# Shift columns in 128-column tiles, and their transpose behind the other pieces of a half step

## The chip, the cores and the metric

The kernel runs on one core of a Trainium2 chip. The core has five engines that run side by side and meet at semaphores: TensorE (PE, matrix products and transposes, with its weight loads PEld), VectorE (DVE), ScalarE (ACT), GpSimd (POOL) and SyncE (SP, which here only issues DMA transfers). The on-chip memory SBUF holds operands; results of TensorE go to PSUM[...]. The metric is the device time of one execution, in microseconds (us), as the median of several runs. Less is better.

## The reference

The input has 8 batches of 512 tokens of width 128. A layernorm is followed by two branches whose results are added to the input: a differential attention with 8 heads, and a mixture of 8 experts of which each token uses two, plus a shared expert.

```python
xn = _layernorm(x)
# attention: two softmaxes per head, each over scores of width F = 8
scores = jnp.einsum('bqhif,bkhif->ibhqk', qs, ks_) * scale
atts = jax.nn.softmax(scores, axis=-1)
att = atts[0] - diff_weight * atts[1]
o = jnp.einsum('bhqk,bkhe->bqhe', att, vs)
normed = (o * rsqrt(mean(o * o) + eps) * norm_w).reshape(b, s, e)
attn = (normed @ Wo.T + bo) * (1.0 - diff_weight)
# experts
gates = jax.nn.sigmoid(xf @ Wg)
vals, idx = jax.lax.top_k(gates, 2)          # then normalized to sum 1
shared = silu(xf @ Ws1) * (xf @ Ws3) @ Ws2
h = silu(einsum('td,edf->tef', xf, We1)) * einsum('td,edf->tef', xf, We3)
routed = einsum('tef,efd,te->td', h, We2, w)
x = x + attn + (shared + routed) / 3
```

A softmax needs the largest score of each row subtracted before the exponential. That maximum is the "shift" of this document.

## The kernel before

**Layout.** For each batch, `qst` and `kst` hold the queries and keys of all heads, stacked in 64 rows per softmax, in two buffers that alternate by batch. Each number is split into an upper and a lower part, and two more rows of `qst` (from row `SHIFT`) hold the negated maximum of every query, so that the product of `kst` and `qst` comes out of TensorE already shifted.

**The main loop** (from line 1066 on) runs over 8 batches x 4 pairs of heads x 4 tiles of 128 keys: 128 steps of two halves. A half step issues, in this order:

1. `scores` (line 764 on): two matmuls into `sc`, which has one PSUM buffer, and ScalarE's exponential, `pe<-sc`.
2. `next_maxima(1)` (line 961): one tile of `maxima`, which runs twelve tiles ahead: two matmuls into `mx` (line 731, one PSUM buffer) and VectorE's `most<-mx` (line 738). Behind the eighth tile of a pair of heads VectorE makes `parts` (lines 741 to 745): the maxima split into an upper and a lower part, 32 columns in all, by four small operations.
3. Transfers that lie ready: an "errand" (a gather or scatter of the experts on GpSimd), a copy into `qst` or `kst`, or the load of an expert's weights.
4. In the first half of a step: `pieces(step)` and then those parts that a piece marked "soon". In the second half: the parts marked "late" and then `weigh`, eight matmuls into `av`.

**Pieces.** All other work is cut into jobs, each a Python generator: the routing, the experts (`pxq`, `ph`, `py`), the shared expert (`ps`), the preparation of a later batch (`px`, `pq`, `pv`), `fold` (`po`), `conclude` (`pn`, `pz`) and `shift` (line 749). A job states for its next piece what it costs and how many PSUM banks it needs. `pieces` (line 1038) sorts the jobs by due time, those with `must` ahead of all, and starts each that still fits: it calls `j.go()`, which issues the piece, and lowers what is left of the room (2.25) and of the three banks of `small_psum`. Only the `shift` jobs have `must`. A bank goes to the tile that asks for it next, and the instruction that first writes it waits until the tile before it has been read. Each engine runs its own instructions in the order in which they were issued.

**The shift.** `shift(b, w)` transposes the 32 columns of `parts` (line 754, `pm`); "late", ScalarE copies the 32 rows to SBUF (line 757, `rows`), and SyncE issues two transfers into rows of `qst` (line 759). They have to be there when the scores of that pair of heads begin, two steps after the piece.

**The rest that the change touches.** `early` takes tiles out of the pool `p12` (twelve wide buffers, tag "w"), which later holds the weights of the experts. `zeros` (line 138) is the source of three small transfers, and `before` (line 938) is a triangular matrix for counting. At the end of the run `combine(b)` loads two results for each token of a batch (`ym`, line 638), adds them to `r` (eight operations of line 647 for each batch), and `settle` stores `r` to the output (line 613, by SyncE) as soon as both sums of a batch are there.

Of the kernel before, what the change touches and what calls it, by code (L numbers as in the profile page):

```python
# [11 lines left out]
F32 = mybir.dt.float32  # L12
# [7 lines left out]
P = 128  # L20
# [11 lines left out]
def kernel(  # L32
# [52 lines left out]
    nc = tc.nc  # L85
    B, S, E = x.shape
    NT = S // P
    NE, _, FF = We1.shape
# [32 lines left out]
    def early(name, *widths):  # L121
        t = p12.tile([P, WIDE], F32, tag="w", name=name)
        begin = [sum(widths[:i]) for i in range(len(widths) + 1)]
        return [t[:, i:j] for i, j in zip(begin, begin[1:])]
# [10 lines left out]
    make_identity(nc, ident)  # L135
    minus_half = const.tile([P, NT], F32, name="minus_half")
    nc.gpsimd.memset(minus_half, -0.5)
    zeros = const.tile([P, E], F32, name="zeros")
    nc.gpsimd.memset(zeros, 0.0)
    wg = const.tile([P, NE], F32, name="wg")  # L140
    nc.sync.dma_start(out=wg, in_=Wg)
# [35 lines left out]
    for i in range(2):  # L177
        vals.append(const.tile([P, NT, H, 32], F32, name=f"vals{i}"))
        qst.append(const.tile([P, H, S], F32R, name=f"qst{i}"))
        kst.append(const.tile([P, H, S], F32R, name=f"kst{i}"))  # L180
    nc.vector.memset(kst[0].bitcast(F32), 1.0)
    nc.gpsimd.memset(qst[0].bitcast(F32), 0.0)

    def later_constants():
# [536 lines left out]
    def maxima(b, w):  # L721

        q, k = qst[b % 2], kst[b % 2]
        most = p2.tile([P, NT, 2, 2], F32, tag="most", name=f"most_{b}_{w}")
        for u in range(2):
            for t in range(NT):
                free = (b, w) == (0, 0) or (b, w, u) == (0, 1, 0)
                tag = "sc" if free and t % 2 else "mx"
                sc = ps_1.tile([P, 2, S], F32, tag=tag, name=f"mx_{b}_{w}_{u}_{t}")
                for i in range(2):  # L730
                    nc.tensor.matmul(  # L731
                        sc[:, i, :],
                        q[ROWS[i], 2 * w + u, t * P : (t + 1) * P],
                        k[ROWS[i], 2 * w + u, :],
                        start=True,
                        stop=True,
                    )
                nc.vector.tensor_reduce(most[:, t, u, :], sc, AX.X, ALU.max, negate=True)  # L738
                latest[:] = [most[0:1, t, u, :]]
                yield  # L740
        parts = p2.tile([P, 2, 2, 2, NT], F32, tag="parts", name=f"parts_{b}_{w}")
        for i in range(2):
            m = most[:, :, :, i].rearrange("p t u -> p u t")
            nc.vector.tensor_copy(parts[:, i, 0].bitcast(F32R), m)
            nc.vector.tensor_tensor(parts[:, i, 1], m, parts[:, i, 0], ALU.subtract)  # L745
        n = 2 * 2 * 2 * NT
        state[b]["parts", w] = parts.rearrange("p i l u t -> p (i l u t)"), n

    def shift(b, w):
        q = qst[b % 2]  # L750
        yield 0.25, 1
        parts, n = state[b].pop(("parts", w))
        pm = small_psum(f"pm_{b}_{w}")
        nc.tensor.transpose(pm[:n, :P], parts, ident)
        yield "late"
        rows = p2.tile([n, P], F32, tag="rows", name=f"rows_{b}_{w}")
        nc.scalar.copy(rows, pm[:n, :P])
        for i in range(2):
            nc.sync.dma_start(
                out=q[64 * i + SHIFT : 64 * i + SHIFT + 2, 2 * w : 2 * w + 2, :].bitcast(F32),  # L760
                in_=rows[n // 2 * i : n // 2 * (i + 1), :],
            )
# [172 lines left out]
            pass  # L935


    before = const.tile([P, P], F32, name="before")
    counted = {}

    def count_up():
# [31 lines left out]
    with tc.manual_schedule():  # L973
        norms = {b: norm(b) for b in range(B)}
        next(norms[0])

        pw = small_psum("pw")
        for i in range(4):
            nc.tensor.transpose(pw[:, i * P : (i + 1) * P], w_raw[:, i, :], ident)

        w_c = const.tile([P, 2, 2, F, H], F32, name="w_c")
        for i in range(2):
            nc.vector.tensor_copy(
                w_c[:, i],
                pw[:, i * P : (i + 1) * P].rearrange("p (u i f) -> p i f u", i=2, f=F),
            )
        w_t = const.tile([P, 2, E], F32, name="w_t")
        nc.scalar.copy(w_t.rearrange("p i e -> p (i e)"), pw[:, 2 * P :])
        run(norms[0])
        first = prepare(0)  # L990
        next(first)
        next(first)
        next(first)
        next(norms[1])
        next(first)
        later_constants()
        run(norms[1])
        px = {1: turn(1)}
        next(norms[2])
        next(first)  # L1000
        next(first)
        run(norms[2])
        run(first)
        later_loads()
        count_up()
        gates(0, state[0]["xnT"])
        for b in range(1, B):
            xnT, p = px.pop(b)
            nc.scalar.copy(xnT, p)
            if b + 2 < B:  # L1010
                next(norms[b + 2])
            if b + 1 < B:
                px[b + 1] = turn(b + 1)
            if b + 2 < B:
                run(norms[b + 2])
            gates(b, xnT)
        nc.scalar.activation(gate.rearrange("p t e -> p (t e)"), pg, AF.Exp, scale=-1.0)
        next_maxima(8)
        run(shift(0, 0))
        sides = const.tile([P, 1], F32, name="sides")  # L1020
        nc.vector.memset(sides, 1.0)
        for i in (32, 96):
            nc.vector.tensor_scalar(sides[i : i + DH], dw[i : i + DH], -1.0, None, ALU.mult)
        keep = const.tile([P, 1], F32, name="keep")
        nc.vector.tensor_scalar(keep, dw, -1.0, 1.0, ALU.mult, ALU.add)
        nw_s = const.tile([P, 1], F32, name="nw_s")
        nc.vector.tensor_scalar(nw_s, nw, keep, None, ALU.mult)
        nc.gpsimd.tensor_scalar(bo_b, bo_b, keep, None, ALU.mult)
        nc.gpsimd.tensor_scalar(s2, s2, OUT_SCALE, None, ALU.mult)
        nc.gpsimd.memset(qst[1].bitcast(F32), 0.0)  # L1030
        nc.gpsimd.memset(kst[1].bitcast(F32), 1.0)
        for b in range(B):
            loads.append(lambda b=b: keep_tokens(b))
        for e in range(NE):
            loads.append(lambda e=e: keep_expert(e))
        next_maxima(AHEAD - 8)

        def pieces(step):

            room, banks = ROOM if step < total else 99.0, BANKS - len(held)  # L1040
            begun = []
            for j in sorted(jobs, key=lambda j: (not j.must, j.last - j.left, j.first)):
                if step < j.first or (j.next is None and not j.ready()):
                    continue
                j.next = j.next or next(j.part)
                cost, need = j.next
                late = step > j.last - j.left
                if need > banks or (cost > room + 0.5 * late and cost > 0 and not (late and begun == [])):
                    continue
                j.go()  # L1050
                room -= cost
                banks -= need
                begun.append(j)
            return begun

        def follow(begun, when):
            for j in begun:
                if j.next == when:
                    j.go()
                    if j.next is None:  # L1060
                        jobs.remove(j)

        total = STEPS * B
        pes = last = None
        step = 0
        while step < total + 1 or jobs or errands or loads:
            for second_half in range(2):
                if step < total:
                    b, r = divmod(step, STEPS)
                    w, c = divmod(r, NT)  # L1070
                    pe = scores(b, w, c, second_half)
                    pes = [pe] if not second_half else pes + [pe]
                next_maxima(1)
                turns += 1
                if errands:

                    if latest:
                        nc.gpsimd.tensor_copy(mark, latest.pop())  # L1078
                    errands.popleft()()

                if copies and (turns % 4 or not loads):
                    copies.popleft()()
                elif loads:
                    loads.popleft()()
                if not second_half:
                    begun = pieces(step)
                    follow(begun, "soon")
                else:
                    follow(begun, "late")
                    if last is not None:  # L1090
                        weigh(*last)
                    last = (b, w, c, pes) if step < total else None
            step += 1
# [48 lines left out]
```

## Time and profile before

| | |
|---|---|
| median of 3 runs | 703.55 us (701.72 to 706.61) |
| the profiled execution | 702.99 us |
| its span, first to last instruction | 701.1 us |
| mean granted TensorE clock | 0.926 of full speed |
| `pm` (line 754): weight load / matmul | 32 x 94 ns / 32 x 283 to 395 ns |
| `parts` (lines 744, 745), each | 64 x 161 to 184 ns, 64 x 166 to 171 ns |
| `rows<-pm` (line 757) | 32 x 238 to 255 ns |
| `most<-mx` (line 738) | 256 x 1222 ns |
| `pe<-sc` (line 776) | 256 x 1024 ns |

A line of the profile's groups names the source line, the engine, the operation and the tiles, output first: `pm<-ident,parts` is the transpose into `pm`. For matmuls "128\*32" means 128 rows by 32 columns of the array. In views that run in order of time the first number is the start in us from the beginning of the span, the second the duration; in brackets stands how long the engine had been idle and which instruction released it. An engine followed by q (SPq) is its instruction queue, here the issue of a transfer. Ends of matmuls are modelled, starts are recorded; so distances between starts are the safer measure.

The maxima's own work is large (312.1 us of VectorE's 500.3), and the shift is small: 32 transposes, 9.2 us of TensorE in all.

### The profile page before, as it was taken

Reading aid. Unit: us, or ns where it says so; the run is one execution under the profiler, and the core shown is the slowest. Engines: PE = TensorE matmul, PEld = TensorE weight load, DVE = VectorE, ACT = ScalarE, POOL = GpSimd, SP = SyncE. Lnnn points to the kernel's source line nnn. Section 1 sums busy time; section 2 is a strip of 40 time slices with the busy share of each in tenths; the row PEclk is TensorE's granted clock in tenths of the full one; section 3 lists DMA queues with packets and bytes.
Section 4 is the critical chain, followed back from the end, with each engine's and each line's share of the span. In section 5 each row is a group of like instructions: output and inputs, shape, how many; then the busy total and the mean of one; then the engine's idle time right before and its main releaser. Section 6 shows DMA issues by size and latency. Waiting matters only on the chain.

```text
span 701.1 us, 10912 instructions
## 1 busy us (share of the span) xinstructions
PE 619.3 (88%) x3788; PEld 329.0 (47%) x3788; DVE 500.3 (71%) x836; ACT 376.2 (54%) x554; POOL 264.1 (38%) x440
## 2 busy tenths in 40 slices
PE   4867768898989999999999999999999999996654
PEld 2733213444525555556545655455555555453113
DVE  7678877678677767867787666777777777777820
ACT  1204425446455675567566755566566666574442
POOL 6313008654034443545245344434544253332000
PEclk9556978999999999999999998999999999998877
DMA  5302313203143344324442444323433444013510
GB/s 163 120 1 90 122 69 93 68 19 122 47 152 111 107 127 145 125 66 136 135 163 77 136 154 143 110 65 105 141 114 112 122 145 114 17 32 114 179 69 16
DMA packets 38696, 72.64 MB, mean 104 GB/s; under 512 B 6489, under 2 KB 12762, under 8 KB 38618
## 3 DMA queue, kind: packets, MB, share of 16 engines
q1 hardware_dynamic: 33026, 61.07, 26.8%
q0 software_dynamic: 4608, 9.45, 4.3%
q10 hardware_dynamic: 1008, 1.44, 0.7%
q8 instruction: 30, 0.49, 0.3%
q14 instruction: 24, 0.20, 0.1%
HBM read 45.68 MB, written 12.09 MB: 82 GB/s over the span
## 4 chain that ended last, share of the span: by engine, by line
PE 66%; DVE 22%; ACT 5%; issue 3%; DMA 2%; POOL 1%; SPq 0%; POOLq 0%; ACTq 0%; DVEq 0%
PE sc L768 12%; PE av L787 12%; DVE most L738 11%; PE ph L570 10%; PE mx L731 8%; PE py L583 5%; PE ps L809 4%; PE pz L877 3%; ACT pe L776 3%; PE pi L393 2%; PE pq L663 2%; PE pg L235 2%; DVE r L647 2%; PE px L225 1%; DVE parts L745 1%
## 5 line engine op out<-in xcount | busy, mean ns | idle before, releaser
L738 DVE TENSOR_REDUCE most<-mx 128x2 f32<-128x1024 f32 x256 | 312.1, 1222 | 119.9 <-PE mx L731 112.9
L776 ACT ACTIVATE pe<-sc 128x1024 f32<-128x1024 f32 x256 | 262.2, 1024 | 221.0 <-PE sc L768 214.6
L768 PE MATMUL sc<-qst,kst 64*128 64x512 f32 x512 | 132.2, 512 | 21.2 <-ACT pe L776 13.9
L787 PE MATMUL av<-pe,vals 128*32 128x512 f32 x1024 | 142.9, 631 | 0.0
L731 PE MATMUL mx<-kst,qst 64*128 64x512 f32 x512 | 123.6, 478 | 14.6 <-DVE most L738 14.5
L768 PEld LDWEIGHTS sc<-qst,kst 64*128 64x128 f32 x512 | 49.2, 188 | 172.0 <-ACT pe L776 119.6
L507 POOL DMA_INDIRECT xq<-tokens,tokens_at x72 | 71.2, 989 | 37.1 <-issue 27.8
L595 POOL DMA_INDIRECT results<-y,results_at x72 | 70.9, 984 | 35.1 <-issue 29.0
L1078 POOL COPY mark<-most 1x2 f32<-1x2 f32 x144 | 25.4, 176 | 149.9 <-DVE most L738 143.8
L570 PE MATMUL ph<-xT,w 128*128 128x128 f32 x576 | 74.4, 283 | 1.5 <-DVE r L881 0.9
L731 PEld LDWEIGHTS mx<-kst,qst 64*128 64x128 f32 x512 | 51.6, 197 | 47.7 <-DVE most L738 45.8
L570 PEld LDWEIGHTS ph<-xT,w 128*128 128x128 f32 x576 | 68.5, 195 | 8.1 <-issue 5.9
L838 POOL TENSOR_TENSOR o<-on 128x128 f32<-128x128 f32 x32 | 14.7, 461 | 142.4 <-DVE on L834 142.0
L787 PEld LDWEIGHTS av<-pe,vals 128*32 128x32 f32 x1024 | 20.7, 109 | 45.6 <-issue 45.4
L809 PE MATMUL ps<-xnT,s 128*128 128x512 f32 x64 | 33.8, 641 | 6.6 <-DVE th_s L544 3.0
L544 DVE SCALAR_TENSOR_TENSOR th<-th,ph 128x512 f32<-128x512 f32 x36 | 24.8, 688 | 19.9 <-ACT th L543 14.2
L583 PE MATMUL py<-w,h 128*128 128x128 f32 x288 | 37.3, 281 | 1.5 <-DVE h L547 0.9
L583 PEld LDWEIGHTS py<-w,h 128*128 128x128 f32 x288 | 33.7, 191 | 5.7 <-issue 3.2
L543 ACT ACTIVATE th<-ph 128x512 f32<-128x512 f32 x36 | 21.5, 597 | 18.8 <-PE ph L570 16.1
L797 ACT ACTIVATE ov<-av,sides 128x512 f32<-128x512 f32 x32 | 22.2, 695 | 12.9 <-PE av L787 12.7
L429 POOL TENSOR_SCALAR here<-numbers,inner 128x128 f32<-128x128 f32 x32 | 19.9, 621 | 15.8 <-DVE inner L381 15.8
L547 DVE TENSOR_TENSOR h<-th,ph 128x512 f32<-128x512 f32 x36 | 24.4, 678 | 0.0
(137 smaller groups left out, 599.0 us busy)
## 6 DMA issues: line engine op xcount, KB each, us to landing
w<-experts SPq DMA_DIRECT2D x72, 384.0 KB
qst<-upper SPq DMA_DIRECT2D x32, 128.0 KB
qst<-lower SPq DMA_DIRECT2D x32, 128.0 KB
kst<-lower SPq DMA_DIRECT2D x32, 128.0 KB
ym<-results SPq DMA_DIRECT2D x16, 256.0 KB
kst<-upper SPq DMA_DIRECT2D x28, 128.0 KB
experts<-in_L_ffn_We_dram SPq DMA_DIRECT2D x24, 128.0 KB
tokens<-xn SPq DMA_DIRECT2D x8, 256.0 KB
```

The lines of the kernel that those rows point to most:

```text
L507: nc.gpsimd.indirect_dma_start(out=xq[:, n, :], out_offset=None, in_=tokens[:, :], in_offset=bass.IndirectOffsetOnAxis(ap=tokens_at[:, j : ...
L544: nc.vector.scalar_tensor_tensor(th, th, 1.0, ph, ALU.add, ALU.mult)
L570: nc.tensor.matmul(ph[:, ns], ws[n][:, f : f + P], xT[:, ns], start=True, stop=True)
L583: nc.tensor.matmul(py[:, ns], hs[c][:, ns], ws[n][:, f : f + E], start=(c == 0), stop=(c == NF - 1))
L595: nc.gpsimd.indirect_dma_start(out=results_of[j], out_offset=bass.IndirectOffsetOnAxis(ap=results_at[:, j : j + 1], axis=0), in_=y[:, n, : ...
L731: nc.tensor.matmul(sc[:, i, :], q[ROWS[i], 2 * w + u, t * P : (t + 1) * P], k[ROWS[i], 2 * w + u, :], start=True, stop=True,)
L738: nc.vector.tensor_reduce(most[:, t, u, :], sc, AX.X, ALU.max, negate=True)
L768: nc.tensor.matmul(sc[:, i, :], kst[b % 2][ROWS[i], 2 * w + u, c * P : (c + 1) * P], qst[b % 2][ROWS[i], 2 * w + u, :], start=True, stop=True,
L776: nc.scalar.activation(pe, sc, AF.Exp, scale=F**-0.5)
L787: nc.tensor.matmul(st["av"][32 * g : 32 * g + 32, :], vals[b % 2][:, c, 2 * w + u, :], pes[u][:, i, :], start=(c == 0), stop=(c == NT - 1),)
L809: nc.tensor.matmul(ph, w[:, c * P : (c + 1) * P], st["xnT"], start=True, stop=True)
L1078: nc.gpsimd.tensor_copy(mark, latest.pop())
```

## The change

Three things change.

- The 32 columns of a pair of heads now stand in one of two fixed tiles `shifts` of 128x128, whose other 96 columns VectorE clears once at the start. The transpose takes the whole tile, so its shape is 128x128; still only the first 32 rows of `pm` are copied on.
- `pieces` still chooses in the same order, but holds back the chosen `must` jobs and starts them after all the others of the half step. They also come last in the list that `follow` goes through for "soon" and "late".
- The tiles `zeros` and `before` come from the pool of wide buffers by `early`, instead of having SBUF of their own.

```diff
-    zeros = const.tile([P, E], F32, name="zeros")
+    (zeros,) = early("zeros", E)
     nc.gpsimd.memset(zeros, 0.0)
...
     nc.vector.memset(kst[0].bitcast(F32), 1.0)
+
+    shifts = [const.tile([P, P], F32, name=f"shifts{i}") for i in range(2)]
+    for t in shifts:
+        nc.vector.memset(t, 0.0)
     nc.gpsimd.memset(qst[0].bitcast(F32), 0.0)
...
-        parts = p2.tile([P, 2, 2, 2, NT], F32, tag="parts", name=f"parts_{b}_{w}")
+        n = 2 * 2 * 2 * NT
+        whole = shifts[w % 2]
+        parts = whole[:, :n].rearrange("p (i l u t) -> p i l u t", i=2, l=2, u=2)
         for i in range(2):
             m = most[:, :, :, i].rearrange("p t u -> p u t")
             nc.vector.tensor_copy(parts[:, i, 0].bitcast(F32R), m)
             nc.vector.tensor_tensor(parts[:, i, 1], m, parts[:, i, 0], ALU.subtract)
-        n = 2 * 2 * 2 * NT
-        state[b]["parts", w] = parts.rearrange("p i l u t -> p (i l u t)"), n
+        state[b]["parts", w] = whole, n
...
         pm = small_psum(f"pm_{b}_{w}")
-        nc.tensor.transpose(pm[:n, :P], parts, ident)
+        nc.tensor.transpose(pm[:, :P], parts, ident)
...
-    before = const.tile([P, P], F32, name="before")
+    (before,) = early("before", P)
...
-            begun = []
+            begun, last = [], []
             for j in sorted(jobs, key=lambda j: (not j.must, j.last - j.left, j.first)):
...
-                j.go()
                 room -= cost
                 banks -= need
-                begun.append(j)
-            return begun
+
+                (last if j.must else begun).append(j)
+                if not j.must:
+                    j.go()
+            for j in last:
+                j.go()
+            return begun + last
```

In the built program of the changed kernel the two memsets stand on VectorE directly behind that of `kst`. On GpSimd the clearing of `qst` moves ahead of the second half of making `ident`. On ScalarE each copy to `rows` stands behind the other late copies of its half step. On SyncE the only change of order is at the end: the two transfers of the last shift stand behind one more store of `r`.

## The prediction

> **What bounds the kernel now.** I read the page first, then the chain that ended last, then TensorE, VectorE and SyncE in order of time around single shifts. The page's busy line and the chain's shares:
>
> ```profile
> PE 619.3 (88%) x3788; PEld 329.0 (47%) x3788; DVE 500.3 (71%) x836; ACT 376.2 (54%) x554; POOL 264.1 (38%) x440
> PE 66%; DVE 22%; ACT 5%; issue 3%; DMA 2%; POOL 1%; SPq 0%; POOLq 0%; ACTq 0%; DVEq 0%
> ```
>
> TensorE bounds most half steps, and VectorE has a fifth of the chain. So each microsecond taken from TensorE has to be checked against VectorE. The view of `parts`, who waited for it:
>
> ```profile
>   PEld pm L754: 14.8, 30
>   PE pm L754: 4.8, 23
> ```
>
> Nearly every shift's transpose stands waiting for its own operand. One shift in order of time, TensorE (start, duration), then an ordinary half step:
>
> ```profile
> 595.48 0.49 PE L731 MATMUL mx<-kst,qst 64*128 64x512 f32 x2
> 596.17 0.28 PE L754 MATMUL pm<-ident,parts 128*32 128x128 f32 x1 [0.20 <-DVE parts L745]
> 596.77 1.98 PE L809 MATMUL ps<-xnT,s 128*128 128x512 f32 x4 [0.32 <-DVE h L547]
> 598.68 0.50 PE L768 MATMUL sc<-qst,kst 64*128 64x512 f32 x2
> 599.02 0.40 PE L731 MATMUL mx<-kst,qst 64*128 64x512 f32 x2
> ...
> 504.63 0.50 PE L731 MATMUL mx<-kst,qst 64*128 64x512 f32 x2
> 505.06 2.05 PE L570 MATMUL ph<-xT,w 128*128 128x128 f32 x16
> 507.04 0.50 PE L768 MATMUL sc<-qst,kst 64*128 64x512 f32 x2
> ```
>
> With no shift the first piece follows `mx` after 0.43 us. With one, `pm` starts after 0.69 and the piece after 1.29. VectorE over the same shift shows why:
>
> ```profile
> 595.95 0.17 DVE L745 TENSOR_TENSOR parts<-most,parts 128x8 f32<-128x8 f32 x1
> 596.03 0.68 DVE L547 TENSOR_TENSOR h<-th,ph 128x512 f32<-128x512 f32 x1
> 596.63 0.25 DVE L832 RECIPROCAL rec<-po 128x16 f32<-128x16 f32 x1
> 596.98 0.42 DVE L834 TENSOR_TENSOR on<-po,rec 128x256 f32<-128x256 f32 x1
> 597.33 1.22 DVE L738 TENSOR_REDUCE most<-mx 128x2 f32<-128x1024 f32 x1
> 598.56 0.69 DVE L544 SCALAR_TENSOR_TENSOR th_s<-th_s,ps 128x512 f32<-128x512 f32 x1
> 599.46 1.23 DVE L738 TENSOR_REDUCE most<-mx 128x2 f32<-128x1024 f32 x1 [0.21 <-PE mx L731]
> ```
>
> `pm` starts 0.05 us after the last `parts`. `ps` starts 0.06 us after `h`, which frees the PSUM bank that `ps` takes when `pm` has taken the one before. The last part of the run is in SyncE's queue:
>
> ```profile
> 664.38 1.82 SPq L638 DMA_DIRECT2D ym<-results  x4
> 666.29 1.33 SPq L759 DMA_DIRECT2D qst<-rows  x2
> 669.24 28.84 SPq L613 DMA_DIRECT2D out_dram<-r  x2
> ...
> 669.28 0.92 PE L768 MATMUL sc<-qst,kst 64*128 64x512 f32 x2 [5.59 <-DMA qst<-rows]
> ...
> 667.03 2.19 DVE L647 SCALAR_TENSOR_TENSOR r<-ym,share,r 128x128 f32<-128x128 f32 x8 [3.12 <-DMA ym<-results]
> ```
>
> The last shift's rows leave at 666.29, and everything after 669.28 hangs on them.
>
> **The change, part by part.** *Moved: 30 transposes in the loop (one is in the prologue, one stands alone at 658.3).* `pm` leaves the place ahead of the pieces, and the bank taken first goes to a piece. In the half step shown, `ps` would start at 595.91 (+0.43), its fourth matmul 1.39 later as in a half step without shift, `pm` 0.43 after that and `sc` 0.21 after `pm` (the distance from `ph`'s last start to `sc`): 597.94 instead of 598.68. That 0.74 us is not what is kept. `mx` at 599.02 must wait for `most`, which ends at 598.55: 598.59. The `most` that follows must wait for `th_s`, which ends at 599.25: 599.27 instead of 599.46. So 0.19 us reaches the next `mx`; VectorE is late next. I did this for all 30, at the following `mx`:
>
> - 8 half steps of this kind (194, 267, 286, 363, 381, 500, 576, 596 us): 0.19 to 0.23, together 1.7.
> - 3 with `py`, where no `th` follows (343, 441, 481): 0.51, 0.74, and 0.07 where `py` itself needs the late `h`: 1.3.
> - 8 in which no bank held the pieces, so only `pm`'s own 0.39 went, of which 0.11 to 0.21 comes back at the end (229, 306, 402, 461, 519, 538, 614, 631): 0.07 to 0.21, together 1.3.
> - 5 short ones (67, 210, 249, 420, 558), where `mx` already waits for `most` (0.05 us apart): 0.
> - 4 with `pi` (115 to 173) and 1 with `ph` waiting for `xT` (325): the piece waits for its own operand, and `pm` now stands behind it: 5 x -0.11 = -0.55.
> - 1 at 90.6, where one bank is held. Before: `pm` at 90.64 after `on`, the two `ps` at 91.23 and 94.49 (after `th_s`), `sc` at 96.50. Now the `ps` take the banks that `on` and `h_s` free, and `pm` is the one that waits for `th_s`: 94.49, `sc` at about 94.8. VectorE is idle there for 3.32 us, so all of it is kept: +1.7.
>
> Sum of the middle: 5.4 us gained.
>
> *The shape.* Weights go from 128x32 (94 ns) to 128x128 (`po`, also a transpose: 145 ns; `ph` 195 ns). Four `po` last 0.60 us and one 0.27, so they start 0.11 us apart: less than the load. The Trainium skill, "TensorE: Matmul & The Clock Gate", section "The mechanism", says that a weight load overlaps matmuls in flight only when its row group differs; all of these use the same rows, so by it 31 x 0.145 = 4.5 us would be lost. The rows show them overlapped; I take 0.11 each, counted above. For the change speaks "TensorEngine Tiling (Array Packing)", section "Key Properties": a change of tiling mode drains TensorE. In the trace a piece that nothing holds starts 0.12 us after a 128x32 `pm` against 0.11 between two 128x128 groups, so that shape is worth 0.01 us there. Only `sc` straight after `pm` at 658 stands 0.58 behind, with the activation ended just before. By the rule at that price, (0.58 - 0.11) x 31 = 14.6 us; by the rows 0.3. I take 0, and up to 2 for the range.
>
> *Added at the start.* Two memsets of 128x128 stand on VectorE between the `kst` memset and the first statistics, which the chain runs through. `kst` took 3.47 us for 4096 columns, so 0.11 each plus a fixed part; small VectorE operations take 0.17, GpSimd's 128x128 memset 0.20. I take 0.3 for both (bounds 0.1 and 0.5). GpSimd now clears `qst` (3.50 us) before it finishes `ident`, so `ident` is ready at about 4.9 instead of 1.4. The first transposes start at 4.38 and would slip 0.5; their reader `w_c` starts at 6.24 behind statistics, which covers it; without that cover it costs 0.5. The prologue's `pm` (49.77) gives back about 0.2, since the 64-row matmul behind it follows after 0.39 us against 0.21. Start: -0.1.
>
> *Pools.* `zeros` and `before` take two of the twelve wide buffers, all taken before the first expert weights; the order of reuse stays the same distance. 0.
>
> *ScalarE and SyncE, the middle.* The copy to `rows` goes behind the other late copies, by 0.5 us (`vals`, `xT`, `y`) to 1.9 (`o` and `xT`). From its end to landing I have the one measured case: 666.29 to 669.14, 2.85 us. The scores follow the copy by 3.55 us or more. The tightest that is delayed is the shift at 153 (copy ends 158.86, `sc` 162.41): 0.14 us would be left. So 0, at a thin margin.
>
> *SyncE, the end.* The last shift's two issues also go behind the late part of the combine begun in the same half step: the store of `r`. It waits for the eight additions that end at 669.22, so it goes at 669.24, and the rows 0.44 later (the distance from one such store at 663.94 to the next issue), 669.68 instead of 666.29. What is queued behind the waiting store is exactly what the last sixteen `sc` matmuls wait for: -3.4 us, with nothing to hide it, as TensorE already stands idle 5.59 us there.
>
> Net: 5.4 - 0.1 - 3.4 = 1.9 us less. On the profiled execution (702.99, span 701.10 with 1.89 around it) this is 701.1. That execution lies 0.56 under the median of the three runs, so against 703.55 I expect 701.6.
>
> **The rivals.** *TensorE keeps its time.* If VectorE's order is not the limit I think (the loss is recovered within a step), the middle keeps what `sc` gains: 9.7 for the shifts, +1.7, -0.55, so 10.9 and net 7.4: 696.1. For it: 88% against 71% busy. Against: in all eight VectorE works without a gap from the first `parts` to the end of `th`, so nothing there can move up.
>
> *The rows come too late, slower than before.* The mechanism is the delayed copy to `rows`; its place the scores of each new pair of heads; the price all that landing takes beyond the slack. It decides where copy to landing exceeds 3.0 us. At 1.2 us more (4.05), the slacks of 0.1 to 0.6 (115 to 194, 249, 558, 614) turn into waits of 0.6 to 1.1 in seven shifts, 5.1 us: net +3.2, 706.8. For it: a measured landing of one case only, in a quiet queue; while expert weights are fetched the queues are fuller. Against: in the trace only the last shift is waited for, though three have no more than 3.56 us from copy to `sc`.
>
> *Nothing changes.* The transposes were covered by work elsewhere and the end costs what the middle brings: 703.5.
>
> **How the numbers follow.** Main case 0.55 (701.6, from 699 to 703.5); TensorE keeps its time 0.17; rows too late 0.18; nothing changes 0.10. About 1% (7 us) is what a measurement of this kernel tells from no change. Faster by over that needs most of the first rival, or a drain that the shape does save: 0.15. Slower by over 1% would need the rows late in most shifts: 0.08. The rest, 0.77, lies within. The range runs from 696 (the first rival's own value) to 707 (the second's).
>
> **What would show it.** Right: `pm` no longer waits for `parts`; a piece follows `mx` by 0.43 in shift half steps; the idle time of TensorE before `mx`, released by `most`, grows; `sc` follows `pm` by 0.21; the scores at 96.5 start about 1.7 earlier; at the end the store of `r` stands ahead of `qst<-rows`, and `sc` waits for that DMA some 9 us instead of 5.6. Wrong: waits of `sc` for `qst<-rows` in the middle, `mx` without new waits while the span falls by 7 us, or a `pm` that takes more than 0.2 us of TensorE.

## The result, and the profile after

| | before | after |
|---|---|---|
| median of 20 runs each | 703.16 us | 699.41 us |
| lowest to highest | 699.75 to 707.14 | 695.50 to 703.74 |
| profiled execution, its span | 702.99, 701.1 | 700.17, 698.4 |

The ratio is 0.994, with a 95% interval of 0.9918 to 0.9962: 2.7 to 5.8 us less, 3.75 by the medians. The forecast was 1.9 us less. The direction and the range held, but the gain is twice the forecast, and several terms of the sum did not hold. Ratios, here and below, leave out slow runs (over 1.5% above the fastest of their kernel: one of e1, one of the kernel before); medians include them.

Single runs spread over 8 us, twice the effect: the profile of one execution shows where time goes, and the medians how much. First the page of after: its busy times, then the shares of the chain that ended last.

```profile
PE 618.0 (88%) x3788; PEld 330.3 (47%) x3788; DVE 498.9 (71%) x838; ACT 376.1 (54%) x554; POOL 263.5 (38%) x440
PE 68%; DVE 21%; ACT 4%; issue 3%; DMA 2%; POOL 1%; ACTq 1%; POOLq 0%; SPq 0%; DVEq 0%
```

Nothing stands out there. The view of the tile `pm` shows the wait that the change was to remove (us, times). The first line is from the idle time of the engine before `pm`, the second from the list of those who waited for it:

```profile
  DVE shifts L751: 1.5, 2
  PEld sc L773: 14.0, 14
```

Before, `pm`'s weight load and matmul stood idle 53 times for the columns, 19.6 us on their two queues; now twice, 1.5 us. The 14.0 us of the scores are hardly a new cost: the copy of `pm` is now often the last operation on ScalarE ahead of them, and so the view names it. Their weight load waits for ScalarE's `pe`, `rows`, `th_s` and `upper` together 137.8 us, and 138.1 before. The half step that the prediction worked out, now on TensorE, then on VectorE:

```profile
590.15 0.49 PE L735 MATMUL mx<-kst,qst 64*128 64x512 f32 x2
590.58 1.99 PE L814 MATMUL ps<-xnT,s 128*128 128x512 f32 x4
592.40 0.27 PE L759 MATMUL pm<-ident,shifts 128*128 128x128 f32 x1
592.60 0.50 PE L773 MATMUL sc<-qst,kst 64*128 64x512 f32 x2
593.26 0.50 PE L735 MATMUL mx<-kst,qst 64*128 64x512 f32 x2 [0.16 <-DVE most L742]
...
592.00 1.21 DVE L742 TENSOR_REDUCE most<-mx 128x2 f32<-128x1024 f32 x1
593.13 0.68 DVE L548 SCALAR_TENSOR_TENSOR th_s<-th_s,ps 128x512 f32<-128x512 f32 x1
593.81 1.23 DVE L742 TENSOR_REDUCE most<-mx 128x2 f32<-128x1024 f32 x1
```

`ps` follows `mx` after 0.43 us (1.29 before), `sc` after 2.45 (3.20), and the next `mx` waits for `most`: VectorE is late next.

To see where the time lies, I set the start of the same exponential (`pe<-sc`, 256 in all) of the two profiles against each other, in us; each column is one execution. The columns of e9 and e8 are for an experiment further down.

| exponential | before | after | after - before | e9 (`pm` first) | e8 (`pm` last) | e8 - e9 |
|---|---|---|---|---|---|---|
| 0 (main loop begins) | 56.47 | 56.83 | +0.36 | 56.84 | 56.84 | 0.00 |
| 20 | 114.43 | 112.28 | -2.15 | 114.90 | 113.83 | -1.07 |
| 48 | 182.25 | 185.01 | +2.76 | 181.71 | 180.99 | -0.72 |
| 148 | 419.93 | 419.70 | -0.23 | 419.36 | 415.83 | -3.53 |
| 152 | 432.21 | 429.16 | -3.05 | 428.81 | 425.30 | -3.51 |
| 240 | 639.66 | 633.49 | -6.17 | 636.46 | 629.62 | -6.84 |
| 248 (last pair of heads) | 670.30 | 667.36 | -2.94 | 662.64 | 655.07 | -7.57 |

Three stretches of "after - before" are not explained by the order of two matmuls: a loss of 4.9 us from 20 to 48, a gain of 2.8 from 148 to 152, and a loss of 3.2 from 240 to 248.

The last one is the predicted one. SyncE, then TensorE, at the end of after:

```profile
663.35 0.34 SPq L617 DMA_DIRECT2D out_dram<-r  x1
663.80 1.33 SPq L764 DMA_DIRECT2D qst<-rows  x2
...
665.84 1.42 PE L773 MATMUL sc<-qst,kst 64*128 64x512 f32 x2 [7.98 <-DMA qst<-rows]
```

The store stands ahead of the rows, and the scores wait 7.98 us instead of 5.59. From the transpose to the issue of the rows it is 11.39 us (652.41 to 663.80); before, 8.02 (658.27 to 666.29). Of the 3.2 us, 2.9 arise there, behind the last shift.

The loss from 20 to 48 lies in the half steps with `pi`. The one near 172, TensorE after:

```profile
171.71 0.51 PE L735 MATMUL mx<-kst,qst 64*128 64x512 f32 x2
173.26 2.74 PE L397 MATMUL pi<-what,here 128*128 128x72 f32 x16 [1.04 <-DVE what L418]
175.80 1.06 PE L867 MATMUL pn<-ident,o 128*128 128x128 f32 x4
176.65 0.42 PE L759 MATMUL pm<-ident,shifts 128*128 128x128 f32 x1
177.00 0.79 PE L773 MATMUL sc<-qst,kst 64*128 64x512 f32 x2
```

`pi` starts 1.55 us behind `mx`, exactly as before. But four `pn` take 1.06 us where they took 0.60, and a pair of `sc` 0.79 where it took 0.50. That is the clock. The next view is of stretches between two moments at which the clock may change (length, then busy time and number of instructions of PE, PEld, DVE, ACT and POOL, then the granted clock, the DMA share and GB/s), first after, then before:

```profile
129.96:133.37 3.41, 2.36 (x18) 1.81 (x18) 3.17 (x10) 1.02 (x1) 0.79 (x2) 1.00 0.00 0
133.37:136.79 3.42, 3.42 (x18) 1.43 (x17) 1.45 (x2) 1.16 (x2) 3.42 (x7) 0.50 0.02 5
150.44:153.85 3.41, 2.36 (x18) 1.83 (x19) 3.27 (x9) 1.32 (x2) 0.00 (x0) 1.00 0.15 56
153.85:157.26 3.41, 3.41 (x17) 2.79 (x16) 0.09 (x1) 0.00 (x0) 0.00 (x0) 0.50 0.00 0
170.92:174.33 3.41, 2.37 (x20) 1.44 (x14) 3.17 (x10) 2.42 (x6) 0.35 (x1) 1.00 0.39 150
174.33:177.75 3.42, 3.42 (x18) 2.84 (x17) 0.70 (x1) 0.00 (x0) 1.34 (x2) 0.50 0.00 0
```

```profile
132.46:135.87 3.41, 2.64 (x21) 2.17 (x21) 2.85 (x8) 0.91 (x1) 1.43 (x3) 1.00 0.00 0
135.87:139.29 3.42, 3.42 (x16) 0.80 (x14) 1.23 (x1) 1.16 (x2) 3.42 (x7) 0.50 0.03 7
152.94:156.35 3.41, 2.64 (x22) 2.22 (x21) 2.90 (x7) 0.95 (x1) 0.00 (x0) 1.00 0.08 28
156.35:159.77 3.42, 3.42 (x26) 1.64 (x25) 1.29 (x2) 2.02 (x4) 0.00 (x0) 1.00 0.00 0
```

After, three stretches with 2.36 or 2.37 us of work in 3.41 are each followed by one at half clock. Before, `pm` stood inside the idle time and the two matching stretches had 2.64: one was followed by half clock, the other was not. From 112 to 190 us the profile of after has four such stretches at half clock (two of them in a row), that of before one. (From 70 to 112 us it is the other way: four in after, six in before.)

### The profile page after: what moved, and what is told of

It is laid out like the page before. It is cut to its first block, busy times and chain, and to the rows that moved or that the text cites. A ratio compares the mean times of both kernels' runs of the same rounds, so it can differ in the third digit from the quotient of the medians.

```text
span 698.4 us, 10922 instructions
## 1 busy us (share of the span) xinstructions
PE 618.0 (88%) x3788; PEld 330.3 (47%) x3788; DVE 498.9 (71%) x838; ACT 376.1 (54%) x554; POOL 263.5 (38%) x440
## 3 DMA queue, kind: packets, MB, share of 16 engines
q0 software_dynamic: 4608, 9.45, 4.5%
## 4 chain that ended last, share of the span: by engine, by line
PE 68%; DVE 21%; ACT 4%; issue 3%; DMA 2%; POOL 1%; ACTq 1%; POOLq 0%; SPq 0%; DVEq 0%
PE av L792 13%; PE sc L773 13%; DVE most L742 11%; PE ph L574 10%; PE mx L735 9%; PE py L587 5%; PE pz L882 3%; ACT pe L781 3%; PE pi L397 2%; PE pq L667 2%; PE ps L814 2%; DVE r L651 2%; PE pg L239 2%; PE px L229 1%; PE po L832 1%
## 5 line engine op out<-in xcount | busy, mean ns | idle before, releaser
L574 PE MATMUL ph<-xT,w 128*128 128x128 f32 x576 | 73.0, 280 | 0.8 <-ACT xT L563 0.7
L574 PEld LDWEIGHTS ph<-xT,w 128*128 128x128 f32 x576 | 67.0, 192 | 7.5 <-issue 5.8
L433 POOL TENSOR_SCALAR here<-numbers,inner 128x128 f32<-128x128 f32 x32 | 19.6, 612 | 13.3 <-DVE inner L385 13.3
```

What stands on the lines that cost most here:

```text
L574: nc.tensor.matmul(ph[:, ns], ws[n][:, f : f + P], xT[:, ns], start=True, stop=True)
```

## The experiments

The theory after the result: (1) the order is all of the gain, the shape nothing; (2) it is partly given back at the end, in SyncE's queue; (3) and partly in the half steps with `pi`, through the clock. Times below are medians; each ratio is to the kernel before on the same chip.

**e1: the order alone.** The kernel before, with only the new `pieces`; columns, shape and pools as before.

> The kernel before with the new order of the pieces alone: the columns keep their 128x32 tile, and zeros and before keep their own SBUF. Theory (the order does everything, the shape nothing, and the start costs the changed kernel 0.4 us): as the changed kernel less 0.4 us, so about 699.0 us, 4 us under the kernel before; the scores of the last pair of heads still wait about 8 us for the rows. Rival (the 128x128 shape saves a drain of TensorE at each of the shifts): 702 us or more, and scores that start more than 0.3 us behind pm. Rival (the order does nothing, the middle is the clock's luck): 703.

700.35 us, ratio 0.9961 (0.9936 to 0.9986), which overlaps the changed kernel's interval; 699.0 was expected. Its profile follows that of after to 0.5 us at the first four rows of the table, and it begins the loop at 56.46 instead of 56.83: this is the cost of the start. The scores of the last pair of heads wait 7.95 us. So the order alone gives a gain of the same kind, and the same losses.

**e2: the shape alone.** The changed kernel with the old `pieces`.

> The changed kernel with the order of before: pm goes first in its half step, in the 128x128 shape. Theory (shape worth nothing, its weight load 0.05 us longer while the pieces wait behind it, the start 0.4 us dearer): 703.2 to 705, that is 0 to 2 us over the kernel before. Rival (the shape saves drains): 701 us or less, and the piece behind pm less than 0.1 us after it.

703.42 us, ratio 1.0001 (0.997 to 1.0031). A piece that nothing holds starts 0.16 us after `pm`, where the 128x32 shape needed 0.12 (the preparation, `pq`, at 535 in e2 and at 538 before). No drain is seen to be saved. The shape and the start do nothing that can be measured, within 2 us.

**e3: the shift's late part first.** Only `pm` is issued last.

```diff
-            return begun + last
+            return last + begun
```

> The changed kernel, but the shift's late part (copy to rows, two transfers) stands ahead of the other late parts again; only pm comes last. Theory (the store of r ahead of the last shift's transfers costs the end 2.9 us): 696.5 us, 2.9 under the changed kernel; the scores of the last pair of heads wait about 5 us for the rows instead of 8. Rival (the scores of the last pair of heads are only waiting where the end would wait anyhow, for the sums): the wait is shorter but the time stays at 699.4.

698.73 us, ratio 0.9937 (0.9913 to 0.9962): it can't be told from the changed kernel. In the profile the rows are issued ahead of the store and the scores wait 6.54 us, 1.4 less, not 3; they still stand behind two stores and four loads. And in this profile TensorE's clock is 0.50 from 656.8 to 694.4, so the end takes longer than in after: 67.2 us from the exponential 240 to the last instruction, against 64.9. The 696.5 us expected did not come; about the price of the store this says nothing, and e6 took its place.

The profile says something else. Its order at `pi` is that of after, but its stretches begin elsewhere (one at 151.65, which lies 1.2 us off the grid of 3.41 us that after's 133.37 is on), and from 112 to 190 us only two are at half clock, not four. From the exponential 20 to 48 it takes 69.9 us, where after takes 72.7 and before 67.8. So what `pi` costs differs from run to run.

**e4: `pm` ahead of `pi` again**, in four half steps.

```diff
-                (last if j.must else begun).append(j)
-                if not j.must:
+                later = j.must and step not in (10, 14, 18, 22)
+                (last if later else begun).append(j)
+                if not later:
```

> The changed kernel, but in the four half steps with pi (near 115, 135, 155 and 175 us) pm keeps the first place. Theory (with pm gone TensorE stands still for 1.05 us in one piece ahead of pi, does less in that stretch of 3.4 us, and the clock is halved for the next one or two stretches, which cost about 1.6, 1.6 and 3 us in three of the four): 695 to 697 us, 2.5 to 4.5 under the changed kernel, and no granted clock of 0.50 between 131 and 185 us, or one stretch at the most. Rival (the phase of the stretches is chance, so that the low clock comes as often): 699.4, within 1 us, with as many low stretches.

698.22 us, ratio 0.9921 (0.9891 to 0.9951). Two half-clock stretches remain from 112 to 190, as against four in after. The theory said at most one, and 2.5 to 4.5 us; it is 1.2 us under the changed kernel, and the intervals overlap. Moving `pm` back leaves most of the idle time: near 131, 0.19 us ahead of `pm` and 0.53 ahead of `pi`, against 1.05 in after. This is the one run that undoes the change in these half steps alone.

**e5: the idle time ahead of `pi` filled.** `pm` stays last; TensorE gets work that computes nothing (four calls, which the trace counts as eight matmuls).

```diff
         pm = small_psum(f"pm_{b}_{w}")
+        if (b, w) in ((0, 3), (1, 0), (1, 1), (1, 2)):
+            for _ in range(4):
+                nc.tensor.matmul(pm[:, :P], ident, ident, start=True, stop=True)
+            yield "filled"
         nc.tensor.transpose(pm[:, :P], parts, ident)
...
-                if not j.must:
+                if not j.must or step in (10, 14, 18, 22):
                     j.go()
```

> The changed kernel with pm last everywhere; in the four half steps with pi, four matmuls of the identity by itself (128x128, result overwritten by pm later) are put into TensorE's idle time ahead of pi. They compute nothing. Theory (the idle time of 1.05 us ahead of pi halves the clock of the next stretches, and that cost 2 to 5 us): no granted clock of 0.50 between 131 and 190 us, 695 to 697 us, 2.5 to 4.5 under the changed kernel. Rival (low stretches there are chance, or do not cost): 699.4, or 700 since the added matmuls delay pi.

695.23 us, ratio 0.9873 (0.9838 to 0.9909), below the changed kernel's interval. Its half step with `pi` and `pn`, then the stretches around it:

```profile
170.60 0.50 PE L735 MATMUL mx<-kst,qst 64*128 64x512 f32 x2
171.04 1.16 PE L761 MATMUL pm<-ident 128*128 128x128 f32 x8
172.15 2.00 PE L397 MATMUL pi<-what,here 128*128 128x72 f32 x16
174.00 0.60 PE L871 MATMUL pn<-ident,o 128*128 128x128 f32 x4
174.43 0.27 PE L763 MATMUL pm<-ident,shifts 128*128 128x128 f32 x1
```

```profile
168.96:172.38 3.42, 3.42 (x26) 1.73 (x23) 2.89 (x10) 3.10 (x6) 0.16 (x1) 1.00 0.50 183
172.38:175.79 3.41, 3.41 (x33) 2.54 (x32) 1.93 (x3) 0.62 (x1) 1.69 (x2) 1.00 0.04 15
```

`pi` still starts 1.55 us behind `mx`, so nothing was moved earlier; `pn` takes 0.60 again, and no half-clock stretch is left between 111 and 636 us. More work for TensorE, and 4.2 us less time: the clock that goes with this idle time is the cause, not the order of the waits. What filling brings is not the price of the change, though: before, too, there was idle time ahead of `pi`, with `pm` in the middle of it.

**e6: the last rows by another queue.** Only for the last shift: copied at once, and issued from ScalarE's queue.

```diff
         nc.tensor.transpose(pm[:, :P], parts, ident)
-        yield "late"
+        end = b == B - 1 and w == 3
+        yield "soon" if end else "late"
...
-            nc.sync.dma_start(
+            (nc.scalar if end else nc.sync).dma_start(
```

> The changed kernel, but the last shift alone copies its rows at once (soon in place of late) and issues its two transfers from ScalarE's queue, where no store stands ahead. Theory (the last scores hang on SyncE's queue, on the store of r and the loads ahead of the rows): the scores' wait of 8 us falls to 2 us or less, and 6 us go from the time: about 693. Rival (the sums of r, finished at 665 us, or a slower clock in the end keep it): wait gone, but 697 or more.

690.37 us, ratio 0.9809 (0.9769 to 0.9849): 9 us under the changed kernel, 3 more than expected. That is more than the change had cost there, since the kernel before waited for these rows too (5.59 us). The earlier copy and the other queue were not tried apart. The end of ScalarE, then TensorE:

```profile
652.17 0.24 ACT L763 COPY rows<-pm 32x128 f32<-32x128 f32 x1
652.44 1.38 ACTq L765 DMA_DIRECT2D qst<-rows  x2
...
656.56 0.50 PE L774 MATMUL sc<-qst,kst 64*128 64x512 f32 x2 [1.12 <-ACT pe L782]
658.18 0.50 PE L774 MATMUL sc<-qst,kst 64*128 64x512 f32 x2
659.82 0.50 PE L774 MATMUL sc<-qst,kst 64*128 64x512 f32 x2 [1.14 <-ACT pe L782]
```

No score waits for the rows any more, and with the 8 us of idle time the half clock that followed it (659.0 to 672.7 in after) is gone too.

**e7: work in the last steps**, against the low clock of the end.

```diff
                     pe = scores(b, w, c, second_half)
+                    if step >= total - 4 and not second_half:
+                        pf = small_psum(f"pf_{step}")
+                        for _ in range(4):
+                            nc.tensor.matmul(pf[:, :P], ident, ident, start=True, stop=True)
```

> The changed kernel with four matmuls of the identity by itself behind the scores in the first half of each of the last four steps; they compute nothing. Theory (the last 31 to 36 us run partly at a halved clock because TensorE does little there): from the first scores behind the wait for rows to the end 29 to 31 us, a granted clock of 1.00 from at most 7 us behind the wait on, 697 to 698.5 us. Rival (ScalarE sets the pace there, and the matmuls only stand in its way): 699.5 to 702.

699.19 us, ratio 0.995 (0.9932 to 0.9969). A miss: the clock's low stretch (662.90 to 673.14) begins before these matmuls, during the wait for the rows, and nothing is gained.

**e8, e9, e10: together.** e8 is the sum of e5, e6 and e7. e10 leaves the matmuls of the last steps out. e9 is e8 with `pm` first in every half step, so that the two differ in the order alone.

> The three together: the changed kernel with the matmuls ahead of pi, the last shift's rows at once and by ScalarE's queue, and the matmuls in the last four steps. Theory (three separate losses): 3, 6 and 1.5 us under the changed kernel, about 689. Rival (they overlap, the end is set by something that stays): 693 or more.

> The kernel with all three additions (e8), but with the order of before: pm goes first among the pieces of its half step. Theory (with the clock ahead of pi and the last rows out of the way, the order alone is worth what the traces show shift by shift: 5.9 us from 200 to 640 us and 1 to 3 us near 90): 692 to 695 us, 6 to 9 over e8. Rival (what TensorE gains in its half step VectorE takes back, as the prediction had it, 3.1 us for the half steps after 190 us and 1.7 at 90): 690 to 691.5. Rival (order worth nothing by itself): 687 or less.

> e8 without the matmuls in the last four steps: the changed kernel with the matmuls ahead of pi and the last rows at once and by ScalarE's queue. Theory (the matmuls at the end do nothing, as e7 gave no gain): within 1 us of 686.3. Rival (once the wait for the rows is gone they hold the clock up): 688 or more.

| | median | ratio to before (95%) |
|---|---|---|
| e8 | 686.28 us | 0.9741 (0.9707 to 0.9774) |
| e9 | 695.56 us | 0.9868 (0.9831 to 0.9905) |
| e10 | 685.92 us | 0.9747 (0.9713 to 0.978) |

e8 came out 2.7 us better than expected: the gains of e5 (4.2) and e6 (9.0) simply add up. e9 is 9.3 us over e8, 8.9 by the ratios, where 6 to 9 was expected. With the idle time at `pi` filled and the last rows out of the way, the order is worth more than twice what the whole change brings (3.75 us). The table above shows it growing evenly from 48 to 240: 6.1 us over 24 shifts, with no jump at 148 to 152 and no half clock in either profile. This part is the order alone. Ahead of 48 and behind 240 the two profiles also differ in their stretches at half clock, so the rest of the 9.3 us is not the order's for certain. Between before and after the same 24 shifts give 6.1 us too, without the 2.8 at 148 to 152. That gain was the clock (before: 0.50 from 422.6 to 429.4) and not the change: e9, with the order of before, takes 9.45 us there, after 9.46, before 12.28. e10 equals e8 within 0.4 us, so e7's part does nothing. e10 is the best version: 17.7 us below the kernel before in its own comparison (703.60).

## Why the forecast held, step by step

**The eight half steps with a held bank: right in kind, too small.** 0.19 to 0.23 us each, 1.7 in all, was the sum; between the two traces they keep 0.31 to 0.43 (for instance -0.75 at the exponential after the shift at 596, +0.40 at the next), together 2.9; e9 and e8 show nearly the same for each. The sum kept `th_s` at its old start. But in the trace of before it started 0.03 us after ScalarE's `th_s<-ps` had ended (598.53, then 598.56); with `ps` earlier it does not wait for that, and starts 2.98 us behind `mx` instead of 3.08. The `most` behind it no longer waits for `mx` either (0.21 us before). The lines of VectorE above show it: `th_s` at 593.13, the next `most` at 593.81, 3.66 us behind `mx` instead of 3.98.

**The other half steps: right on the whole.** `py`: 0.74 forecast at 441 and 0.74 in the trace, but 0.38 for 0.51 at 343 and 0.12 for 0.07 at 481. The unheld ones keep 0.17 to 0.34, one of them (631) nothing, together 1.5 where 1.3 was said. The one at 90.6: 1.7 forecast; the exponential behind it starts 1.61 earlier, counted from the one ahead of it. With the held ones, the 24 shifts from 194 to 631 give 6.1 us, where the prediction's terms for them add up to 4.2.

**The shape: right.** The rule on draining modes gave 14.6 us gained, that on weight loads 4.5 lost, the rows 0.3; e2 has nothing, to within 2 us.

**The start: too small.** A cost of 0.1 was forecast, 0.36 measured. The two memsets took 0.31 as said; the 0.2 that the prologue's `pm` should give back did not come: the matmul behind it follows after 0.41 us, against 0.32 before (the prediction had read 0.39).

**The end: right mechanism, a little smaller.** The issue of the rows moved back by 3.37 us behind the transpose, 3.4 was forecast. But from issue to scores it took 2.04 us instead of 2.99, so the end loses 2.4 to 2.9. This also bears on the rival of late rows: no score waits for them in the middle, as the prediction held.

**The half steps with `pi`: a term was left out.** The prediction wrote "5 x -0.11 = -0.55" because `pm` now stands behind a piece that waits for its own operand. At full clock that is right: from e9 to e8 three of these half steps lose 0.10 to 0.18 us. It left out that `pm` broke TensorE's idle time, and with it the clock. Over all the traces, 13 stretches hold ten or more of `pi`'s 16 matmuls and 2.36 or 2.37 us of work, all of them with `pm` last and nothing filled in: each was followed by half clock. (In the first of the four half steps, with 2.49 to 2.58 us of work, one of five was.) With `pm` inside the idle time (2.64 to 2.69 us of work; before, e2, e4) it was 3 of 7, and with the idle time filled none. In the pair of profiles 4.9 us went there from the exponential 20 to 48. How much it is on average is not settled: e4, which takes back only this, gains 1.2 us, with overlapping intervals. e5's 4.2 us is more than the price, since filling helps with `pm` first as well: e2 and e9 have the same order and differ by 7.9 us, 5.1 of them behind the exponential 240, which leaves some 2.7 for the filling (an estimate).

The Trainium skill, "TensorE: Matmul & The Clock Gate", section "What's actually happening", describes a free-running window of 3.41 us: every half-clock stretch here inside the run lasts 3.41 us or a whole multiple, which agrees. It has the clock fall after an idle window; here it fell after windows in which TensorE worked 69% of the time, and the measurement decides. The share of busy time is not the whole rule either: see the last section.

So the net came out in range with errors on both sides, and in part by luck: the middle gains more than forecast, and a loss that was not forecast takes some of that away. Put together from the traces, 6.1 for the 24 shifts, 1.6 at 90.6, -0.4 at the start and -2.4 to -2.9 at the end make 4.4 to 4.9 us (an estimate); the 3.75 measured leaves about 1 us for the clock at `pi`, near e4's 1.2. The two profiles alone would mislead: their spans differ by 2.7 us, and 2.8 of that is the half clock which before happened to have near 422. The first rival (TensorE keeps its time, 10.9 us in the middle) was too generous, since VectorE does take back about half of each gain in the held half steps (0.75 at first, 0.31 to 0.43 kept); e8 gains 7.6 us on e9 up to the last pair of heads, between that and the 5.4 of the forecast. That nothing changes is excluded by the interval.

Much of the spread of 8 us between runs goes with the clock, whose mean was taken for each run. Of the 20 runs of after, the five with 0.934 to 0.936 took 696.1 to 698.7 us, the two with 0.916 took 703.3 and 703.7. (Three with 0.952 to 0.967 took 695.5 to 702.5 and form a line of their own; e10's profile, with 0.976, lacks the half clock that the other profiles have from about 20 to 60 us.) The six runs of e5 lie within 3.3 us. Still open: why stretches at half clock appear near 422 us in some profiles (before, e1, e3, e7) and not in others of the same order. The stretches do not begin at the same point of the program in each run, which would explain it, but no run was made that sets that point.

## What to carry to other kernels

When an instruction leaves an idle stretch of TensorE, count not only its time but what it did there: taking it out can make one long wait of two short ones and cost a stretch of half clock. Look for what the last work of the run hangs on, and in which queue it stands; getting a transfer of a few KB out from behind a store that waits was worth as much (9 us) as all the reordering in the loop. And where an effect is half as large as the spread of single runs, compare the traces at matching instructions, check the clock of each before a difference is put down to the change, and test the order in a kernel in which the other losses are gone.

## What the hardware showed

- In after, each of the three stretches with `pi` and 2.36 us of work in 3.41 was followed by half clock. But the stretch from 167.51 on, with 2.30 us, none of it `pi`, was not. Over all the traces, 44 stretches at full clock between 66 and 640 us have 2.28 to 2.39 us of work: the 13 with ten or more matmuls of `pi` were all followed by half clock, the 31 others never. `pi` has 72 columns where `sc`, `mx` and `av` have 512; that narrow matmuls count for less would fit, but no run tested it. Four matmuls that compute nothing ahead of each of four `pi`, 1.16 us each time, bought back 4.2 us.
- A wait of 8 us near the end costs more than itself: in after, the clock stays at half until 672.7, 6.8 us past the start of the scores that had waited, and e6, without the wait of 7.98 us, gains 9.0. In the profiles of e3 and e4 it stays at half until 694 and 697.
- A transpose of 128x128 with 96 empty columns costs TensorE 0.04 us more than one of 128x32 in front of a piece (0.16 from start to start against 0.12).
